# Layer 1's dilated 3x3 convolution by row differences: four products per two output rows, in groups of six rows

## The chip, the cores and the metric

The kernel runs on one core of a Trainium2 chip. The metric is the device time in microseconds of one execution; a kernel's time is the median of several runs. All data are fp32.

## The reference, cut to what matters

Two layers run one after the other on 32 images of 128 channels and 56 x 56 pixels. Layer 0 is a depthwise 7x7 convolution, a layer norm, and a mixture of 8 experts with two experts per pixel and a limited capacity; its result is the image plus the normalized value plus the experts' output. Layer 1, the only one that the change touches, is:

```python
feat = conv2d(x, conv_w, padding=DIL, dilation=DIL)      # 3x3, dilation 3, 128 -> 64 channels
feat = batchnorm(feat, bn1_g, bn1_b, bn1_m, bn1_v)
feat = jax.nn.gelu(feat, approximate=False)
F2 = jnp.fft.fft2(feat.astype(jnp.float32), axes=(-2, -1))
...
attn = complex_softmax(attn)                             # 8 heads of 8 channels
out_f = jnp.abs(jnp.fft.ifft2(out_f, axes=(-2, -1)))
...
gate = cg * F2
gate = jnp.abs(jnp.fft.ifft2(gate, axes=(-2, -1)))
y = jnp.concatenate([out_f, gate], axis=1)
return y + x
```

Output row h of the convolution needs the input rows h - 3, h and h + 3, and in each of them the columns w - 3, w and w + 3.

## The kernel before, in words

Layer 0 writes three things to DRAM: the normalized rows (xf), the experts' outputs in the order of the experts' slots (yf), and, for each pixel, two slot numbers that stay in SBUF. Layer 1 begins when the last expert is done. It works on 16 pairs of images; image pr and image pr + 16 lie in the two halves of the 128 partitions (2 x 64 output channels).

Four parts run in layer 1, written as Python generators whose `yield w` tells how many columns of PE work have just been issued:

- `release` (L428) issues one gather on GpSimd's queue: for 128 pixels, one of the two expert outputs, by an indirect DMA (L444). A gather waits for the PE instruction that was current 16 gathers earlier (`leash`). `total` (L451) adds, for a block of 8 image rows of both images, the two gathered tiles to the tile `xa` by two VectorE additions (L460), and stores the sum to DRAM. Its loads and stores go over SP's queue. `worked` (L468) counts the columns issued and releases a gather per PACE columns (L1510). `bring` (L476) makes sure that a block of rows is summed, which issues what is missing at once, and loads it back.
- `front` (L1264) is the convolution of one pair. `place` (L1249) transposes a block of the sums on PE and adds it to the padded input tile `xp` of each image (L1260); rows of `xp` are RP = 59 elements apart. `taps` (L1267) then issues, for a group of 8 output rows, 9 taps x 2 images of matmuls (L1271) with 448 columns; the two images go to the two halves of the PSUM tile `pf`, so that they use the two column halves of the array. ScalarE applies batch norm and gelu in one pass (L1279).
- `back` (L1339) is all the rest of one pair: the transforms, the attention and the outputs. `transform` (L1306) takes banks of four 128-column blocks: four PE transposes (L1314), a copy of the bank to `mid` on VectorE (L1301), four products with a constant matrix (L1322), and a copy of the result on ScalarE (L1325). It is used four times per pair (rows forward, columns forward, columns back, rows back). `attended` (L1419) and `absolute` (L1483) add the input to the results (L1427, L1490) and store them.
- The main loop (L1512 to L1538) runs `back` of one pair and feeds it steps of the next pair's `front`, in proportion to the work done; the first sixth of `back` gets none except where `back` asks for some. The framework then orders each engine's instructions by estimated readiness, so neighbours in the code can be some places apart on an engine.

[...] PSUM has five banks shared by transposes, products and attention, two for `pf` and one for the Gram matrix.

Lines that the change and the prediction touch: L436 (buffers of `xa`), L485 (loading `xp`), L1230 (the convolution's weights `cw`), L1249 to L1296, L1306 to L1337, L1427, L1490, L1507 to L1510. L1369 is the square root of the Gram matrix's diagonal: it runs once per pair and serves as a mark in time.

Of the kernel before, what the change touches and what calls it, by code (L numbers as in the profile page):

```python
# [30 lines left out]
F32 = mybir.dt.float32  # L31
# [43 lines left out]
def conv_seq_kernel(ctx: ExitStack, tc: tile.TileContext, t: dict, out: bass.AP, dbg: dict):  # L75
# [352 lines left out]
    def release():  # L428

        n = made_["asked"]  # L430
        if n >= NRB * NG:
            return
        made_["asked"] += 1
        r, k = divmod(n, NG)
        if k == 0:
            xs = d6.tile([128, NB, C], F32, name="xa", tag="xa")  # L436
            nc.sync.dma_start(out=xs, in_=xfv[:, r * NB : (r + 1) * NB, :])
            begun_[r] = xs, []
        if k % NB == 0:
            begun_[r][1].append(d6.tile([128, NB, C], F32, name="y"))  # L440
        m = k % NB
        s = (slot1, slot2)[k // NB]
        marks.append(step["pe"])
        gated(marks[max(0, n - leash["n"])], nc.gpsimd.indirect_dma_start(  # L444
            out=begun_[r][1][-1][:, m, :],
            out_offset=None,
            in_=yf[: 1 + reach(r), :],
            in_offset=bass.IndirectOffsetOnAxis(ap=s[:, r * NB + m : r * NB + m + 1], axis=0),
        ))
# [33 lines left out]
        nc.sync.dma_start(out=xs, in_=xsv[:, r * NB : (r + 1) * NB, :])  # L483

    def inputs(pr):  # L485
        xps = [d4.tile([C, XL], F32, name="xp") for i in range(2)]
        for i in range(2):
            nc.sync.dma_start(out=xps[i], in_=t["xp"][pr + i * HI])
        return xps

    def ahead(i, of):

# [23 lines left out]
    if True:  # L516
# [620 lines left out]
        for e in range(E):  # L1137
            todo = late
            chain["on"] = e >= E - 3
            if e + 1 < E:  # L1140
                todo = todo + [due(1.4, lambda e=e: scale(e + 1))]
            if e in pairs:
                todo = todo + search(*pairs[e])
            if e == E - 1:
                for s in late + [left]:
                    s()
                left = lambda: None
                locate()
                lists_.close()
                rkey.__exit__(None, None, None)  # L1150
                d4 = ctx.enter_context(tc.tile_pool(name="d4", bufs=4))
                d6 = ctx.enter_context(tc.tile_pool(name="d6", bufs=6))
                d3 = ctx.enter_context(tc.tile_pool(name="d3", bufs=3))
                first_inputs = inputs(0)
                todo = []
            if e + 1 < E - 1:
                ids2, gates2 = lists()
                steps, late = listing(e + 1, ids2, gates2)
                todo = todo + steps
            elif e + 1 < E:  # L1160
                (ids2, gates2), late = last, []
            if e == E - 4:
                last = lists()
                steps, done_ = listing(E - 1, *last)
                todo = todo + steps + done_
            slots_ = len(chunks) * 4 - 6
            state = [0, 0, 0.0, 0]
            whole = sum(share.get(f, 0.7) for f in todo)

            def tick():  # L1170
                state[0] += 1
                if e == E - 1:
                    state[2] += 1
                    ahead(i, state[2])
                with tc.issue_after(step["dve"].ins):
                    while state[1] < len(todo) and state[2] * slots_ < state[0] * whole:
                        s = todo[state[1]]
                        if s in apart and state[3] == state[0]:
                            break
                        s()  # L1180
                        state[2] += share.get(s, 0.7)
                        state[1] += 1
                        state[3] = state[0]

            for i, c0 in enumerate(chunks):
                if i + 1 < len(chunks):
                    then = fetch(ids, chunks[i + 1], e == E - 1)
                elif e + 1 < E:
                    then = fetch(ids2, 0, e + 1 == E - 1)
                if e in (E - 3, E - 2):  # L1190
                    for n in range(2):
                        if 2 * (i + (e - E + 3) * len(chunks)) + n < NC:
                            put(0, 2 * (i + (e - E + 3) * len(chunks)) + n)
                state[2] = 0 if e == E - 1 else state[2]
                left = expert(e, c0, gates, *now, tick, left)
                now = then
            assert state[1] == len(todo)
            if e + 1 < E:
                ids, gates = ids2, gates2
# [5 lines left out]

    d1 = ctx.enter_context(tc.tile_pool(name="d1", bufs=1))
    d2 = ctx.enter_context(tc.tile_pool(name="d2", bufs=2))
    ring = ctx.enter_context(tc.tile_pool(name="ring", bufs=6))
    psum = ctx.enter_context(tc.tile_pool(name="psum_d", bufs=5, space=PSUM))
    psumf = ctx.enter_context(tc.tile_pool(name="psum_f", bufs=2, space=PSUM))  # L1210
    psum1 = ctx.enter_context(tc.tile_pool(name="psum_g", bufs=1, space=PSUM))
# [16 lines left out]
        return scale, shift  # L1228

    cw = load(d1, "cw", [C, 9, DD], t["conv_w"])  # L1230
    bsc, bsh = batchnorm("bn1")


# [15 lines left out]
    def place(r, xps):  # L1249
        xs, rb = rows.pop(r), r % NB  # L1250
        for m0 in range(0, NB, 4):
# [3 lines left out]
            for m in range(nm):  # L1255
                nc.tensor.transpose(pv[:, :, m, :], xs[:, m0 + m, :], ident)  # L1256
            for i in range(2):
                px = interior(xps[i], rb * P8, P8)[:, :, m0 * P8 : (m0 + nm) * P8]
                pi = pv[:, i * P8 : (i + 1) * P8].rearrange("p r m s -> p r (m s)")
                step["dve"] = nc.vector.scalar_tensor_tensor(  # L1260
                    out=px, in0=pi, scalar=bC, in1=px, op0=ALU.add, op1=ALU.add
                )

    def front(pr, xps, feat):  # L1264


        def taps(pf, g, k0):  # L1267
            for k in range(k0, k0 + 3):
                o = ((k // 3) * 3 + 8 * g) * RP + (k % 3) * 3
                for i in range(2):  # L1270
                    step["pe"] = nc.tensor.matmul(  # L1271
                        pf[i * DD : (i + 1) * DD, : 8 * W],
                        lhsT=cw[:, k, :],
                        rhs=xps[i][:, o : o + 8 * RP].rearrange("p (h w) -> p h w", w=RP)[:, :, :W],
                        start=(k == 0),
                        stop=(k == 8),
                    )
            if k0 == 6:
                nc.scalar.activation(  # L1279
                    feat[:, 8 * g * W : 8 * (g + 1) * W], pf[:, : 8 * W], AF.Gelu, scale=bsc, bias=bsh  # L1280
                )

        bring(pr * NB)
        bring(pr * NB + 1)
        place(pr * NB, xps)
        bring(pr * NB + 2)
        yield NB * 64
        for g in range(NB):
            if g + 1 < NB:
                place(pr * NB + g + 1, xps)  # L1290
                bring(pr * NB + g + 3)
                yield NB * 64
            pf = psumf.tile([128, 512], F32, name="pf")
            for k0 in (0, 3, 6):
                taps(pf, g, k0)
                yield 3 * 8 * W  # L1296

# [3 lines left out]
    act = nc.scalar.copy  # L1303
    K2 = 2 * KF

    def transform(src, n, m, by, to, copy, more=None):  # L1306

        M = by.shape[1]

        def turn(i0):  # L1310
# [2 lines left out]
            for i in range(ni):  # L1313
                step["pe"] = nc.tensor.transpose(pt[:m, i * 128 : (i + 1) * 128], src(i0 + i), ident)  # L1314
            mid = ring.tile([128, 4, 128], F32, name="mid")
            dve(mid[:m, :ni, :].rearrange("p i c -> p (i c)"), pt[:m, : ni * 128])
            return i0, ni, mid

        def product(i0, ni, mid):
# [19 lines left out]
    def back(pr, xps, feat):  # L1339
# [79 lines left out]
        def attended(g):  # L1419
# [1 line left out]
            root = bank("root")  # L1421
            nc.scalar.activation(root[:, : 8 * W], feat[:, 8 * g * W : 8 * (g + 1) * W], AF.Sqrt)
            for i in range(2):
                oa = ring.tile([128, 8 * W], F32, name="oa", tag="o")
                ov = oa[:DD].rearrange("p (h w) -> p h w", w=W)
                rv = root[i * DD : (i + 1) * DD, : 8 * W].rearrange("p (h w) -> p h w", w=W)
                nc.vector.tensor_tensor(out=ov, in0=rv, in1=interior(xps[i], 8 * g, 8)[:DD], op=ALU.add)  # L1427
                nc.sync.dma_start(out=out[pr + i * HI, :DD, 8 * g : 8 * g + 8, :], in_=ov)


# [39 lines left out]
        for i, w in enumerate(  # L1470
            transform(
                lambda k: Z[:, k, :], KF, 4 * KF, ih,
                lambda k, n: T4[:, 2 * k * H : 2 * (k + n) * H], act,
            )
        ):
            if i % 2 and i // 2 < NB:
# [6 lines left out]
        def absolute(at, pm):  # L1483
            j0, nj = at
            nc.scalar.activation(pm, pm, AF.Abs)
            for i in range(2):
                ob = ring.tile([128, 8 * W], F32, name="ob", tag="o")
                ov = ob[DD:].rearrange("p (b j w) -> p b j w", b=2, w=W)
                px = xps[i][DD:, INT0 : INT0 + H * RP].rearrange("p (b j w) -> p b j w", b=2, w=RP)
                nc.vector.tensor_tensor(  # L1490
                    out=ov,
                    in0=pm[i * DD : (i + 1) * DD].rearrange("p (j b w) -> p b j w", b=2, w=W),
# [5 lines left out]

        yield from transform(
            lambda j: T4[:, bass.DynSlice(j, 4 * KF, step=NT)], NT, 4 * KF, iw,  # L1500
            lambda j, n: (j, n), absolute,
        )

    MAIN = 2 * (NT * (64 + 4 * KF) + KF * (64 + 4 * KF)) + NT * 128 + NB * 16 * W + 2 * -(-KF // 4) * 2 * KF
    FRONT = NB * (NB * 64 + 9 * 8 * W)  # L1507
    LEAD = MAIN // 6
    leash["n"] = 16
    PACE = (MAIN + FRONT) / (2 * NP) * 1.07  # L1510
# [152 lines left out]
```

## Time and profile before

| | us |
|---|---|
| median of 3 runs | 5322.87 (5310.27 to 5332.21) |
| the profiled execution, its own time | 5289.68 |
| its span | 5287.9 |
| PE busy in the span | 4697.6 |
| DVE busy | 2808.8 |
| ACT busy | 2112.7 |
| GpSimd (POOL) busy | 2611.9 |
| first and last convolution matmul of layer 1, start | 2988.5 and 5212.8 |

Engines in a profile are PE (TensorE's matmuls), PEld (its weight loads), DVE (VectorE), ACT (ScalarE), POOL (GpSimd) and SP (the queue that issues DMAs). A line such as `L1271 PE MATMUL pf<-xp,cw 128*64 128x448 f32 x4032 | 916.6, 562 | 8.4` reads: line 1271, engine and operation, output and inputs, shape, count, busy time of the group in us, mean length of one in ns, idle time of the engine just before them in us. An fp32 matmul shows as two instructions. PE's ends are modelled, so who reads a PSUM tile tells more about when it was done. "remote" or "unknown queue" marks a wait whose end the records do not attribute.

The busy tenths in 40 slices (132 us each) show layer 0's convolution in the first five slices, the routing and the experts up to slice 22, and layer 1 from slice 23 on.

### The profile page before, as it was taken

The page shows a single profiled execution, that of the slowest core. Times are in us where ns is not written, and L with a number is a line of the kernel's source. Part 1 is how long each engine was busy: PE and PEld are TensorE (multiplying, and loading weights), DVE is VectorE, ACT ScalarE, POOL GpSimd, SP SyncE. Part 2 cuts the span into 40 slices and gives each one's busy share as a digit, 9 for nine tenths or more (in the row PEclk, how much of TensorE's full clock was granted, in tenths as well). Part 3 has the DMA queues.
Part 4 walks back from the last instruction along what each step waited for, and adds up shares of the span by engine and source line. Part 5 has one row for each costly group of instructions (what it writes and reads, how often), then busy time and mean ns, then how long its engine had stood idle before and what let it go on. Part 6 is the DMA issues. An engine that isn't in the chain of part 4 may idle for free.

```text
span 5287.9 us, 87255 instructions
## 1 busy us (share of the span) xinstructions
PE 4697.6 (89%) x32984; PEld 3233.7 (61%) x32984; DVE 2808.8 (53%) x5777; ACT 2112.7 (40%) x4260; POOL 2611.9 (49%) x2633
## 2 busy tenths in 40 slices
PE   8888835999999999999999899989999888888899
PEld 7677724777777777666666455555555554455556
DVE  4787876667676766341112245545545444444456
ACT  3676751444444444443444233333333222222234
POOL 0000022555554555666636666666666666666660
PEclk9999966999999999999999899999999999999999
DMA  9988940222222222333356545555565555555552
GB/s 261 267 258 252 269 110 25 68 63 65 63 67 63 65 66 64 85 91 88 90 165 159 141 120 158 157 153 160 157 163 158 157 159 152 132 150 153 152 147 60
DMA packets 767256, 705.23 MB, mean 133 GB/s; under 512 B 72752, under 2 KB 679089, under 8 KB 762741
## 3 DMA queue, kind: packets, MB, share of 16 engines
q1 hardware_dynamic: 596580, 487.54, 31.1%
q0 software_dynamic: 81664, 167.15, 14.4%
q10 hardware_dynamic: 88592, 44.96, 3.0%
q8 instruction: 262, 4.29, 0.3%
q14 instruction: 158, 1.29, 0.1%
HBM read 472.99 MB, written 226.39 MB: 132 GB/s over the span
## 4 chain that ended last, share of the span: by engine, by line
PE 72%; DVE 10%; ACT 5%; another core or an unknown queue 4%; issue 4%; DMA 3%; POOL 0%; SPq 0%; ACTq 0%; DVEq 0%; POOLq 0%
PE py L1064 17%; PE pf L1271 15%; PE ph L1049 15%; PE pm L1322 9%; PE pt L1314 4%; PE pg L1346 2%; PE pxt L1031 2%; DVE st L196 2%; ACT y L222 2%; DVE y L231 2%; DMA xf<-y 2%; PE psa L171 2%; ACT hT L1052 2%; PE pre L1411 2%
## 5 line engine op out<-in xcount | busy, mean ns | idle before, releaser
L444 POOL DMA_INDIRECT y<-yf,slot x1568 | 1559.3, 994 | 918.8 <-issue 364.2
L1025 POOL DMA_INDIRECT xg<-xf,ids x861 | 907.2, 1054 | 797.9 <-PE ph L1049 510.6
L1052 ACT ACTIVATE hT<-ph,b1t 128x512 f32<-128x512 f32 (+1 forms) x992 | 658.0, 682 | 1219.4 <-PE ph L1049 1048.2
L1064 PEld LDWEIGHTS py<-W,hT 128*128 128x128 f32 x7872 | 967.5, 196 | 242.9 <-ACT hT L1052 139.0
L1064 PE MATMUL py<-W,hT 128*128 128x128 f32 x7872 | 1039.4, 285 | 63.4 <-ACT hT L1052 49.9
L1271 PE MATMUL pf<-xp,cw 128*64 128x448 f32 x4032 | 916.6, 562 | 8.4 <-issue 5.6
L1049 PE MATMUL ph<-xT,W 128*128 128x512 f32 (+1 forms) x1984 | 896.2, 591 | 4.1 <-issue 3.7
L1080 DVE TENSOR_TENSOR yo<-py,b2t 128x512 f32<-128x512 f32 (+2 forms) x256 | 170.7, 669 | 894.6 <-issue 525.7
L1301 DVE COPY mid<-pt 112x512 f32<-112x512 f32 (+3 forms) x480 | 311.1, 662 | 594.8 <-PE pt L1314 228.7
L1049 PEld LDWEIGHTS ph<-xT,W 128*128 128x128 f32 x1984 | 355.5, 191 | 338.2 <-issue 333.7
L1271 PEld LDWEIGHTS pf<-xp,cw 128*64 128x64 f32 x4032 | 283.4, 138 | 437.7 <-issue 398.9
L217 POOL TENSOR_SCALAR y<-y,sd,nb 128x128 f32<-128x128 f32 x49 | 25.5, 540 | 690.8 <-PE plq L263 689.9
L1325 ACT COPY T<-pm 128x464 f32<-128x464 f32 (+2 forms) x240 | 123.5, 520 | 495.2 <-PE pm L1322 315.5
L1090 ACT ACTIVATE yo<-yo,gates 128x128 f32<-128x128 f32 (+1 forms) x984 | 312.4, 394 | 11.4 <-DVE yo L1080 5.7
L222 ACT ACTIVATE y<-y,nb,sd 128x128 f32<-128x128 f32 x735 | 287.5, 481 | 30.9 <-DVE nb L209 30.9
L171 PE MATMUL psa<-xt,stay 112*64 112x98 f32 (+1 forms) x4608 | 230.9, 260 | 39.4 <-DVE y L179 23.6
L1260 DVE SCALAR_TENSOR_TENSOR xp<-pxs,beta,xp 128x256 f32<-128x256 f32 x448 | 173.4, 445 | 154.7 <-PE pxs L1256 47.6
L1322 PE MATMUL pm<-ih,mid 116*128 116x112 f32 x928 | 152.9, 314 | 109.3 <-DVE mid L1301 56.3
L171 PEld LDWEIGHTS psa<-xt,stay 112*64 112x64 f32 (+1 forms) x4608 | 217.4, 145 | 48.4 <-DVE y L179 25.7
L460 DVE TENSOR_TENSOR xa<-xa,y 128x896 f32<-128x896 f32 x224 | 243.4, 1087 | 3.2 <-DVE mid L1301 0.4
L1322 PEld LDWEIGHTS pm<-ih,mid 116*128 116x128 f32 x928 | 131.4, 218 | 180.4 <-DVE mid L1301 59.7
L1279 ACT ACTIVATE feat<-pf,bn_shift,bn_scale 128x448 f32<-128x448 f32 x112 | 81.1, 724 | 401.8 <-remote 152.2
(409 smaller groups left out, 6180.6 us busy)
## 6 DMA issues: line engine op xcount, KB each, us to landing
xt<-in_x_dram SPq DMA_DIRECT2D x256, 392.0 KB
yf<-yo SPq DMA_DIRECT2D x240, 256.0 KB
xp<-in_xp_dram SPq DMA_DIRECT2D x32, 1832.0 KB
xa<-xf SPq DMA_DIRECT2D x112, 448.0 KB
xsum<-xa SPq DMA_DIRECT2D x112, 448.0 KB
xs<-xsum SPq DMA_DIRECT2D x112, 448.0 KB
xf<-y ACTq DMA_DIRECT2D x42, 1024.0 KB
y<-yf,slot POOLq DMA_INDIRECT x1568
```

The costliest lines, as they stand in the source:

```text
L171: nc.tensor.matmul(ps[h * 64 : (h + 1) * 64, c * TG : (c + 1) * TG], lhsT=wts[b][:, c4 + c, :], rhs=xv[: PKS[b], c, h, :, b * NB : b * NB ...
L222: nc.scalar.activation(yi, yi, AF.Identity, scale=sd[:, i : i + 1], bias=nb[:, i : i + 1])
L444: gated(marks[max(0, n - leash["n"])], nc.gpsimd.indirect_dma_start(out=begun_[r][1][-1][:, m, :], out_offset=None, in_=yf[: 1 + reach(r), :],
L460: nc.vector.tensor_tensor(out=xs, in0=xs, in1=y, op=ALU.add)
L1025: paced(q, nc.gpsimd.indirect_dma_start(out=xg[:n, q, :], out_offset=None, in_=xf, in_offset=bass.IndirectOffsetOnAxis(ap=ids[:n, c0 + q : ...
L1049: step["pe"] = nc.tensor.matmul(ph[:, :ns], lhsT=W1[:, e, f * C : (f + 1) * C], rhs=xT[:, :ns], start=True, stop=True)
L1052: gelu = nc.scalar.activation(hT[:, f, :ns], ph[:, :ns], AF.Gelu, bias=b1t[:, e, f : f + 1])
L1064: step["pe"] = nc.tensor.matmul(py[:n, q * C : (q + 1) * C], lhsT=hT[:, f, q * 128 : q * 128 + n], rhs=W2[:, e, f, :], start=(f == 0), sto ...
L1090: nc.scalar.activation(yo[:n, q], yo[:n, q], AF.Copy, scale=gates[:n, c0 + q : c0 + q + 1])
L1271: step["pe"] = nc.tensor.matmul(pf[i * DD : (i + 1) * DD, : 8 * W], lhsT=cw[:, k, :], rhs=xps[i][:, o : o + 8 * RP].rearrange("p (h w) -> ...
L1301: step["dve"] = nc.vector.tensor_copy(to, of)
L1322: step["pe"] = nc.tensor.matmul(pm[:, i * M : (i + 1) * M], lhsT=mid[:m, i, :], rhs=by, start=True, stop=True)
```

## The change

For outputs y(h) and y(h + 3) the four input rows r0 = x(h - 3), r1 = x(h), r2 = x(h + 3) and r3 = x(h + 6) are needed. With the three kernel rows k0, k1 and k2, four products take the place of six:

- m0 = k0 (r0 - r2), m1 = (k0 + k1 + k2)/2 (r1 + r2), m2 = (k0 - k1 + k2)/2 (r2 - r1), m3 = k2 (r3 - r1)
- y(h) = m0 + m1 + m2 and y(h + 3) = m1 - m2 + m3

Each product still has three column taps and runs over three rows at a time (rows h, h + 1, h + 2), so a group is six output rows. A pair has nine such groups and one of the last two rows. Row sums and differences are made on VectorE for both images at once (`lift`), into five buffers; the two mixed kernel rows are made once. PSUM holds m1 and m2 in one bank and m0 and m3 in another; ScalarE copies the first to `feat`, three VectorE operations combine them (m1 is added to both side products, then m2 is added to one and subtracted from the other), and the gelu runs on `feat` in place. Besides, `xp` becomes one tile for both images; `xa` has four buffers instead of six; the output tiles have five buffers of their own instead of six; in the two inverse transforms every second copy to `mid` goes to ScalarE; and FRONT, from which PACE follows, is reckoned anew.

```diff
@@ release
-            xs = d6.tile([128, NB, C], F32, name="xa", tag="xa")
+            xs = d4.tile([128, NB, C], F32, name="xa", tag="xa")
@@ weights, once
+    mixed = d1.tile([C, 2, 3, DD], F32, name="mixed")
+    cu = [cw[:, 0:3, :], mixed[:, 0], mixed[:, 1], cw[:, 6:9, :]]
+    nc.vector.tensor_tensor(out=cu[2], in0=cu[0], in1=cu[3], op=ALU.add)
+    nc.vector.tensor_tensor(out=cu[1], in0=cu[2], in1=cw[:, 3:6, :], op=ALU.add)
+    nc.vector.tensor_tensor(out=cu[2], in0=cu[2], in1=cw[:, 3:6, :], op=ALU.subtract)
+    nc.vector.tensor_scalar(out=mixed, in0=mixed, scalar1=0.5, scalar2=None, op0=ALU.mult)
@@ front
+    SEED = {0: (0, 6, ALU.subtract), 1: (6, 3, ALU.add), 2: (6, 3, ALU.subtract), 3: (9, 3, ALU.subtract)}
-        def taps(pf, g, k0):
-            for k in range(k0, k0 + 3):
-                o = ((k // 3) * 3 + 8 * g) * RP + (k % 3) * 3
-                for i in range(2):
-                    step["pe"] = nc.tensor.matmul(
-                        pf[i * DD : (i + 1) * DD, : 8 * W],
-                        lhsT=cw[:, k, :],
-                        rhs=xps[i][:, o : o + 8 * RP].rearrange("p (h w) -> p h w", w=RP)[:, :, :W],
...
+        def lift(g):
+            n, ms = lines(g)
+            k = n * RP + 3
+            tt = {}
+            for m in (1, 2, 0, 3)[: len(ms)]:
+                tt[m] = d5.tile([128, 2, SL], F32, name="tt")
+                a, b, op = SEED[m]
+                at = [(GR * g + r) * RP for r in (a, b)]
+                step["dve"] = nc.vector.tensor_tensor(
+                    out=tt[m][:, :, :k], in0=xps[:, :, at[0] : at[0] + k], in1=xps[:, :, at[1] : at[1] + k], op=op
+                )
+            return tt
+        def taps(g, tt):
...
+            for pair_ in ((1, 2), (0, 3)):
+                pf = psumf.tile([128, 512], F32, name="pf")
+                for j, m in enumerate(pair_):
...
+                    for k in range(3):
+                        for i in range(2):
+                            step["pe"] = nc.tensor.matmul(
+                                pf[i * DD : (i + 1) * DD, j * 3 * W : j * 3 * W + nw],
+                                lhsT=cu[m][:, k, :],
+                                rhs=tt[m][:, i, 3 * k : 3 * k + n * RP].rearrange("p (h w) -> p h w", w=RP)[:, :, :W],
+                                start=(k == 0),
+                                stop=(k == 2),
+                            )
...
+                nc.scalar.copy(od, mid_)
+                nc.vector.tensor_tensor(
+                    out=side, in0=side, in1=od[:, 0:1].broadcast_to([128, 2, nw]), op=ALU.add
+                )
+                nc.vector.tensor_tensor(out=od[:, 0], in0=side[:, 0], in1=od[:, 1], op=ALU.add)
+                step["dve"] = nc.vector.tensor_tensor(out=od[:, 1], in0=side[:, 1], in1=od[:, 1], op=ALU.subtract)
+            nc.scalar.activation(od, od, AF.Gelu, scale=bsc, bias=bsh)
...
+            lifted.append((g, lift(g)))
+            if len(lifted) == 2:
+                k = lifted.pop(0)
+                taps(*k)
+                yield load_of(k[0])
@@ transform
-            dve(mid[:m, :ni, :].rearrange("p i c -> p (i c)"), pt[:m, : ni * 128])
+            (act if shared and i0 % 8 else dve)(mid[:m, :ni, :].rearrange("p i c -> p (i c)"), pt[:m, : ni * 128])
@@ outputs
-                oa = ring.tile([128, 8 * W], F32, name="oa", tag="o")
+                oa = outs.tile([128, 8 * W], F32, name="oa", tag="o")
@@ pacing
-    FRONT = NB * (NB * 64 + 9 * 8 * W)
+    FRONT = NB * NB * 64 + sum(load_of(g) for g in range(NGR))
```

## The prediction

> **What bounds the kernel now.** I read the page first (engine shares, slices, chain), then the chain by time from 2850 us on, then cut layer 1 into windows at the square root of the norms (L1369, once per image pair, first at 3080.7 us, last at 5230.7), then one stretch of the timeline.
>
> ```profile
> PE 4697.6 (89%) x32984; PEld 3233.7 (61%) x32984; DVE 2808.8 (53%) x5777; ACT 2112.7 (40%) x4260; POOL 2611.9 (49%) x2633
> ...
> PE   8888835999999999999999899989999888888899
> ...
> DVE  4787876667676766341112245545545444444456
> ...
> PE 72%; DVE 10%; ACT 5%; another core or an unknown queue 4%; issue 4%; DMA 3%; POOL 0%; SPq 0%; ACTq 0%; DVEq 0%; POOLq 0%
> ...
> L1271 PE MATMUL pf<-xp,cw 128*64 128x448 f32 x4032 | 916.6, 562 | 8.4 <-issue 5.6
> ```
>
> The convolution pf is the largest piece of PE in layer 1 (slices 23 to 40), and PE holds 72% of the chain.
>
> ```profile
> 3189.10 6.92 PE pf L1271 x36
> ...
> 3543.39 12.54 another core or an unknown queue
> ...
> 5206.79 6.92 PE pf L1271 x36
> ```
>
> 36 instructions in 6.92 us: 192 ns from one to the next (562 is the length of one; two images run side by side in the two column halves). One pair has 7 x 9 x 2 = 126 matmuls, each two instructions: 252 x 192 = 48.4 us.
>
> ```profile
> 2988.50:3080.70 92.20, 81.88 (x433) 42.93 (x434) 23.77 (x52) 12.69 (x20) 58.73 (x61) 0.92 0.49 117
> 3080.70:3898.10 817.40, 750.77 (x4472) 453.39 (x4471) 418.43 (x717) 261.94 (x439) 517.73 (x517) 0.96 0.59 158
> 3898.10:5105.10 1207.00, 1047.83 (x5963) 631.64 (x5962) 569.06 (x969) 348.77 (x585) 771.72 (x779) 0.94 0.57 152
> 5105.10:5230.70 125.60, 122.83 (x747) 74.16 (x745) 64.84 (x115) 43.56 (x74) 27.99 (x30) 0.99 0.30 75
> 5230.70:5287.90 57.20, 46.06 (x295) 34.41 (x293) 40.90 (x70) 30.67 (x56) 0.00 (x0) 0.94 0.24 57
> ```
>
> Columns: length, then busy time of PE, PEld, DVE, ACT, POOL, then granted clock, DMA share, GB/s. Six pairs take 136.2 us each with 86 gathers each (517 / 6), eight take 150.9 with 97 or 98, and the pair that has few gathers left takes 125.6. So PE sets the pace, and gathers with their company cost 10 to 25 us a pair on top. The later pairs are those where the lead in gathers is used up.
>
> ```profile
> 3539.43 6.99 PE L1271 MATMUL pf<-xp,cw 128*64 128x448 f32 x36
> ...
> 3541.18 2.21 DVE L460 TENSOR_TENSOR xa<-xa,y 128x896 f32<-128x896 f32 x2
> ...
> 3541.51 1.57 POOL L444 DMA_INDIRECT y<-yf,slot  x1 [0.30 <-issue]
> ...
> 3547.14 0.94 POOL L444 DMA_INDIRECT y<-yf,slot  x1 [0.30 <-issue]
> ...
> 3552.41 0.72 ACT L1279 ACTIVATE feat<-pf,bn_shift,bn_scale 128x448 f32<-128x448 f32 x1 [13.12 <-remote]
> 3555.95 2.00 DVE L1301 COPY mid<-pt 116x512 f32<-116x512 f32 x3 [12.56 <-remote]
> ```
>
> Two things to see. The activation can read the last pf only at 3552.41, 6 us after the record says that PE was done: the "unknown queue" of the chain is PE itself, slower than its records after a long dense run, with the granted clock at 0.94 on the mean. And a gather takes POOL 0.94 + 0.30 us, but 1.57 under DVE's addition of two SBUF tiles.
>
> [...] The nearest row here is layer 0's convolution, also two column halves:
>
> ```profile
> 319.10 5.50 PEld L171 LDWEIGHTS psa<-xt,stay 112*64 112x64 f32 x128
> ```
>
> 128 loads, each with a matmul of 98 columns, in 5.50 us: 43 ns apiece. So 64-column weights don't hold a short matmul at 98 columns, still less at 168.
>
> **The change part by part.**
>
> PE. Per group of six rows 4 products x 3 taps x 2 images = 24 matmuls of 168 columns; nine groups, and a last one of 18 with 112. That is 216 x 2 = 432 instructions and 36 shorter. Scaling 192 ns by columns gives 72, scaling psa's 43 gives 74; I take 73, and 49 for the short ones: 31.5 + 1.8 = 33.3 us. PE saves 48.4 - 33.3 = 15.1 us a pair, 242 over 16. Bounds: 72 ns saves 15.5; if each load's 138 ns were serial, PE would lose 13 a pair, which psa excludes.
>
> DVE. Added per pair: [...] 9 side additions of 336 elements in PSUM (L1416 has 618 ns for 448, so 0.50), 4.5; 18 additions of 168 and 2 of 112 at about 0.32, 6.4. Removed: 7 of 30 mid copies, 4.4. DVE overlaps neighbours by some 0.08 us per instruction (59 more per pair, 4.9), so DVE goes from 69.7 (418.43 / 6) to about 69.7 + 31.3 - 4.4 - 4.9 = 92 us a pair, from half of the time to three quarters. It lies beside PE. Not everywhere: in the two inverse transforms DVE already writes 28 outputs of 0.62 us and all mid copies, and a difference in front of a mid copy delays the PE products that wait for it. In the changed instruction order most differences stand in fours before and in attention; in the inverse stages single ones stand between copies. I take 2 us a pair, bounds 0 and 10.
>
> ACT. Nine copies of 336 (L1325 has 546 ns for 464, so 0.44) and one short, 4.2; seven mid copies, 3.7; ten gelus for seven, about 1; table loads go from 7 to 10 per pair in the instruction order, 3 x 1.3 = 3.9. ACT rises from 43.7 (261.94 / 6) to 56 us of 125. Hidden, except that ACT now waits for DVE before a gelu, and behind it are the copies of T and Z that PE waits for. Within the 2 us above.
>
> POOL. The number of gathers is the same. Each costs 1.30 us with its issue (996 ns mean + 0.30): 98 are 127 us. Excess over 0.94 is about 5 us a pair now, under 14 additions (L460) and 4 gatings (L1460, 1.12), 19 us of two-input DVE work; the differences add 20 us of that kind, so another 4 to 5. POOL then needs 132 us in a late pair, 116 in an early one. Against PE's 150.9 - 15.1 = 136 this leaves almost nothing. Behind a late gather stand L460's addition in DVE's order, and behind that the copies. I take 4 us in a late pair, bounds 0 and 13.
>
> Pacing. One gather per amount of work, in the same proportion (PACE scales with FRONT), but the first front is shorter work, so the lead starts some 8 gathers smaller; in the changed order 14 additions per pair begin at the sixth interval instead of the seventh. One pair moves from early to late.
>
> Buffers. xa from 6 to 4: rows are 20 us apart, so a store has landed, nothing. Output tiles have five buffers instead of six: up to 1 us in a pair, in the 2 us above. Weights mixed once: four DVE instructions before the first product, under 2 us, beside transposes. SP's DMAs are as many, in the same turn.
>
> Sum: 92.2 - 5 (DVE is busy in the first front: additions, placing, differences) + 5 x (136.2 - 15.1 + 2 = 123) + 9 x (150.9 - 15.1 + 4 = 140) + (125.6 - 15.1 + 1.5 = 112) + 56 = 2130 us where layer 1 has 2299.4. That is 169 less. The profiled execution took 5289.68 us (span 5287.9), 33 under the median of the runs, 5322.87; against that median I get 5153.
>
> **The rivals.**
>
> (a) PE's saving arrives whole[...]. For: 125.6 us in a pair without many gathers, DVE's idle time. Against: POOL's 132. 242 + some 10: 5070. Chance 0.22.
>
> (b) POOL and DVE become the bound of the late pairs: 147 instead of 140, early 130. For: 127 us of POOL stretched to 150.9 already. 87 + 650 + 1323 + 118 + 57 = 2235, 64 less: 5259. Chance 0.21, of which 0.06 reach no change.
>
> (c) Slower: the ring PE, ACT copy, DVE side addition, ACT gelu in every group. [...] while DVE waits for the side product, the mid copies behind it wait, and PE with them. A group saves PE 1.5 us; from 1.5 us of stall per group the change loses. At 2 us, 0.5 x 160 groups = 80 more: 5403. For: waits of PE for mid copies total 55.5 us before pm alone. Against: a group is used one group later, and five PSUM banks lie between. Chance 0.13.
>
> (d) It doesn't do what it says: short matmuls at 138 ns. 5530; psa speaks against it. Chance 0.02.
>
> **How the numbers follow.** Forecast 0.42, with its own range 5110 to 5200. What a measurement can tell from no change is 0.5%, 27 us. Faster: 0.42 + 0.22 + 0.15 = 0.79; same 0.06 and 0.01 of (c), 0.07; slower 0.14. The range goes from 5050, under (a), to 5320, where 0.17 of (b), (c) and (d) stay out above and 0.03 below.
>
> **What would show it.** 432 pf instructions per pair at 73 ns in runs of 24; DVE at 85 to 95 us a pair; early pairs near 123 and late near 140; gathers longer on the mean than 996 ns; POOL over 90% with its issue in late pairs. Wrong if the differences wait in front of mid copies so that PE's idle time before pm doubles, or if pf spacing is over 100 ns.

## The result, and the profile after

The kernel after takes 5509.22 us (median of 4 runs, 5495.98 to 5516.82), the kernel before 5322.03 (4 runs, 5310.27 to 5332.21): a ratio of 1.035, interval 1.032 to 1.038. The change makes it 3.5% slower, where 3% faster was forecast. The later runs fell on four chips (8, 12, 13 and 15 by their numbers; that of this first comparison isn't known). On three of them the kernel before takes 5284 to 5321 us, on number 12 it took 4836, in one run; each run below is therefore compared with its neighbours on the same chip.

The windows of the kernel after, cut as those of before (first product of layer 1, first square root of the norms, pairs, the pair that has few gathers left, the tail; columns as there):

```profile
3014.30:3098.20 83.90, 65.29 (x643) 58.29 (x644) 46.72 (x107) 16.30 (x29) 50.55 (x46) 0.85 0.45 112
3098.20:3833.00 734.80, 608.34 (x4808) 483.58 (x4806) 456.22 (x899) 277.33 (x482) 447.12 (x435) 0.90 0.55 148
3833.00:5327.10 1494.10, 1140.94 (x8651) 904.00 (x8652) 839.10 (x1643) 504.31 (x865) 910.91 (x881) 0.85 0.53 139
5327.10:5439.70 112.60, 106.43 (x955) 85.99 (x954) 83.81 (x172) 56.02 (x97) 16.77 (x16) 1.00 0.30 72
5439.70:5494.20 54.50, 43.24 (x295) 33.35 (x293) 37.05 (x63) 33.67 (x63) 0.00 (x0) 0.97 0.27 60
```

Five pairs take 147.0 us each, nine take 166.0, and the pair with few gathers takes 112.6. Read the fourth row first: with 16 gathers instead of 98, the new convolution gives 112.6 where the old one, with 30, gave 125.6. There the forecast of 112 is met. In the rows with gathers the same work takes up to 53 us longer, and the granted clock falls to 0.85 (before: 0.94). From the first square root to the last the kernel after needs 2341.5 us and before 2150.0: the first five pairs lose 55, the next nine 149, the last gains 13. Another 17 us were lost ahead of the first square root; that is layer 0, which the change doesn't touch and which took 26 us longer in this execution, less 8 us gained in the lead-in.

The page of the kernel after, engine shares, slices and chain:

```profile
PE 4618.8 (84%) x36440; PEld 3557.0 (65%) x36440; DVE 3160.1 (58%) x6757; ACT 2302.2 (42%) x4625; POOL 2662.8 (48%) x2633
...
PE   8888836999999999999987788887778777777879
...
PEclk9999958999999999999999899988888878888889
...
PE 66%; DVE 11%; issue 7%; ACT 7%; another core or an unknown queue 5%; DMA 3%; POOL 0%; SPq 0%; DVEq 0%; ACTq 0%; POOLq 0%
```

PE's busy time is only 79 us less, for an estimated 242 us of removed products, and from slice 23 on it is no longer full: sevens and eights. No other engine is full either, and "issue" and "unknown queue" (together 8% of the chain before) are 12%: time that ends with nobody's recorded work. One stretch of the timeline shows such a piece:

```profile
5075.23 1.93 PE L1316 MATMUL pf<-tt,mixed 128*64 128x168 f32 x24
...
5080.98 0.94 POOL L444 DMA_INDIRECT y<-yf,slot  x1 [0.30 <-issue]
5082.23 0.95 POOL L444 DMA_INDIRECT y<-yf,slot  x1 [0.30 <-issue]
5083.48 0.96 POOL L444 DMA_INDIRECT y<-yf,slot  x1 [0.30 <-issue]
5084.75 0.94 POOL L444 DMA_INDIRECT y<-yf,slot  x1 [0.30 <-issue]
5085.80 0.44 ACT L1332 COPY feat<-pf 128x336 f32<-128x336 f32 x1 [12.72 <-remote]
5086.00 0.94 POOL L444 DMA_INDIRECT y<-yf,slot  x1 [0.31 <-issue]
...
5086.29 1.10 PE L1316 MATMUL pf<-tt,cw 128*64 128x168 f32 x5 [9.13 <-issue]
```

By the records the 24 products of m1 and m2 are done at 5077.16. ACT, whose next instruction is the copy of them, starts it 8.6 us later; PE does nothing for 9.13 us; and all that while POOL issues one gather after the other, 0.30 us apart. That is the pattern that the experiments are about. I call it a late hand-over. Where hand-overs are counted below, the lateness of one is the start of the ACT or DVE instruction that first reads a PSUM bank, less the recorded end of the products in it or of the reader's own last instruction, whichever is later (in layer 1 the banks pf, pt, pm, pre and pim are counted); over 2.5 us it counts as late.

### The profile page after: what moved, and what is told of

Its sections match the earlier page's. It is cut to its first block, busy times and chain, and to the rows that moved or that the text cites. A ratio compares the mean times of both kernels' runs of the same rounds, so it can differ in the third digit from the quotient of the medians.

```text
span 5494.2 us, 95680 instructions
## 1 busy us (share of the span) xinstructions
PE 4618.8 (84%) x36440; PEld 3557.0 (65%) x36440; DVE 3160.1 (58%) x6757; ACT 2302.2 (42%) x4625; POOL 2662.8 (48%) x2633
## 3 DMA queue, kind: packets, MB, share of 16 engines
q0 software_dynamic: 81664, 167.15, 13.7%
## 4 chain that ended last, share of the span: by engine, by line
PE 66%; DVE 11%; issue 7%; ACT 7%; another core or an unknown queue 5%; DMA 3%; POOL 0%; SPq 0%; DVEq 0%; ACTq 0%; POOLq 0%
PE py L1064 16%; PE ph L1049 14%; PE pf L1316 11%; PE pm L1384 8%; PE pt L1376 3%; PE pg L1408 2%; PE pxt L1031 2%; ACT y L222 2%; PE pre L1473 2%; DVE st L196 2%; DVE y L231 2%; PE psa L171 2%; ACT hT L1052 2%; PE pxs L1265 2%
## 5 line engine op out<-in xcount | busy, mean ns | idle before, releaser
L444 POOL DMA_INDIRECT y<-yf,slot x1568 | 1613.0, 1029 | 1061.8 <-issue 363.7
L1316 PE MATMUL pf<-tt,cw 128*64 128x168 f32 (+1 forms) x3648 | 403.2, 341 | 219.6 <-issue 104.6
L1316 PEld LDWEIGHTS pf<-tt,cw 128*64 128x64 f32 x3648 | 300.5, 152 | 288.1 <-issue 154.6
L1316 PE MATMUL pf<-tt,mixed 128*64 128x168 f32 (+1 forms) x3840 | 376.2, 324 | 46.2 <-issue 25.2
L1299 DVE TENSOR_TENSOR tt<-xp 128x360 f32<-128x360 f32 (+1 forms) x624 | 298.9, 518 | 155.8 <-remote 69.3
L1363 DVE COPY mid<-pt 112x512 f32<-112x512 f32 (+2 forms) x368 | 244.9, 668 | 215.3 <-PE pt L1376 83.2
L1316 PEld LDWEIGHTS pf<-tt,mixed 128*64 128x64 f32 x3840 | 278.4, 144 | 138.5 <-issue 87.9
L1332 ACT COPY feat<-pf 128x336 f32<-128x336 f32 x144 | 63.1, 438 | 532.8 <-remote 254.9
```

Source lines behind the costliest of these rows:

```text
L1299: step["dve"] = nc.vector.tensor_tensor(out=tt[m][:, :, :k], in0=xps[:, :, at[0] : at[0] + k], in1=xps[:, :, at[1] : at[1] + k], op=op)
L1316: step["pe"] = nc.tensor.matmul(pf[i * DD : (i + 1) * DD, j * 3 * W : j * 3 * W + nw], lhsT=cu[m][:, k, :], rhs=tt[m][:, i, 3 * k : 3 * k ...
L1363: step["dve"] = nc.vector.tensor_copy(to, of)
```

## The experiments

The theories, by the numbers that the expectations use: (1) the saving is lost only together with the gathers, by the row differences contending with them; (2) the ring PE, ACT copy, DVE addition, gelu stalls; (2') POOL is full, and what waits is waiting for gathers; (3) ACT's copies and table loads (1283 ns each in the traces of before and after) or the fewer buffers cost it; (5) while gathers run, PE's results reach the other engines late, whoever needs the gathers.

**Without gathers, and without either added part.** No gather, zeros in the additions (both kernels):

```diff
-        gated(marks[max(0, n - leash["n"])], nc.gpsimd.indirect_dma_start(
...
+            begun_[r][1].append(made_["zero"])
```

The kernel after without the differences, and, as another run, without the combining operations:

```diff
-                tt[m] = d5.tile([128, 2, SL], F32, name="tt")
...
+                tt[m] = GR * g * RP + SEED[m][0] * RP
...
-                                rhs=tt[m][:, i, 3 * k : 3 * k + n * RP]
+                                rhs=xps[:, i, tt[m] + 3 * k : tt[m] + 3 * k + n * RP]
```

```diff
-                nc.scalar.copy(od, mid_)
-                nc.vector.tensor_tensor(
...
-            nc.scalar.activation(od, od, AF.Gelu, scale=bsc, bias=bsh)
+            nc.scalar.activation(od, mid_[:, :nr], AF.Gelu, scale=bsc, bias=bsh)
```

> Leaves out the gathers of the kernel before: the additions read a tile of zeros instead, everything else stays. Theory 1 (what the change loses is lost only together with the gathers): PE then sets every pair, some 124 us each as in the pair with few gathers, 2990 + 85 + 15 x 123 + 57 = 4980, between 4930 and 5060. Theory 2 (the loss is in the convolution's own ring from PE to ACT to DVE to ACT): the same value; this run is the base for the next one.

> Leaves out the gathers of the kernel after in the same way. Theory 1: the saving of PE arrives: pairs of 108 to 113 us, 4790 in all, at least 150 less than the kernel before without gathers. Theory 2: the ring stalls with or without gathers: pairs of 125 us or more, 4980 or more.

> The kernel after, but the products read the input rows themselves: leaves out the row sums and differences. 20 us of two-input VectorE work a pair are gone, the gathers stay. Theory 1 in the form that the differences contend with the gathers: below 5300, near 5200. Theory 2: the ring stays, so at least 5400. Theory 3 (ACT's copies, table loads, fewer buffers): at least 5400 as well.

> The kernel after, but the gelu reads the bank of m1 and m2 straight from PSUM: leaves out the ACT copy and the VectorE additions that combine the four products. Theory 2 (the ring): below 5300, near 5200. Theory 1 (differences against gathers): 5400 or more, only the 11 us a pair of DVE work from PSUM, which has no second SBUF input, are gone.

Measured, all on the chip where the kernel before takes 4835.68: 4793.49, 4656.14, 4827.41 and 4870.59. Without gathers a good half of the saving arrives: 137 us of the 242, the pairs fall from 121 to 112. (Theory 1 had asked for 150 at least, and 4980 had been expected of the first run, as this chip's time wasn't known.) The other two can't be read without the kernel after beside them, hence the controls:

> The kernel after, unchanged, beside the kernel before, since the kernel before took 4836 us beside the four runs so far and not 5322. Where the kernel before takes about 5320 here, 5500 is expected. Where it takes about 4836: theory 1 (the saving is lost to the gathers on any machine state) expects 4950 to 5010, 3% above; theory 5 (what is lost is late PE work, which the traces at 4836 do not show) expects 4870 to 4890, since the runs without the differences and without the combining additions took 4827 and 4871 and each leaves something out; a saving that arrives would be 4650 to 4700.

> The kernel before, unchanged, for its trace on the same chip as the run beside it. At about 4836 in all: pairs of 121 to 128 us, no granted half clock inside the dense stages, and the activation that reads pf starts where the record of the last pf ends. At about 5320: as in the trace of before that is known.

5476.58 (5466.91 to 5499.91) against 5283.79 (5268.53 to 5302.67), ratio 1.037, interval 1.032 to 1.041; the kernel before with its trace 5272.86. The slow-down is there on a second chip, and with it the late hand-overs. Then the three cut kernels again, beside the kernel after:

> The kernel after without its gathers (the additions read zeros), once more, to stand beside the kernel after of the same call. If the kernel before takes about 5290 beside it: theory 1 (everything that the change loses is lost only while gathers run) expects 4660, as where the kernel before took 4836, since no PE work is then recorded late; a slower chip as such would give 5000 or more.

> The kernel after without the row sums and differences. Where the kernel before takes 4836, POOL ran its gathers back to back all through layer 1 and 4827 came out; the same is expected there. Where the kernel before takes 5290: if the differences beside the gathers are what is lost (theory 1), 5250 or less; if the loss is that each hand-over from PE to ACT and DVE comes late while gathers run (theory 5), 5350 to 5450.

> The kernel after without the ACT copy and the VectorE additions that combine the products: two fewer hand-overs per group. Where the kernel before takes 4836: 4870 again. Where it takes 5290: theory 5 (late hand-overs) 5300 or less, nearer to it than the run without the differences; theory 1, 5400 or more.

> The kernel after, unchanged, with its trace, as the base of the three runs before. Where the kernel before takes 5290: 5480. Where it takes 4836: POOL as the bound (98 gathers of 1.33 us are 130 us a pair) gives 2915 + 15 x 129 + 57 = 4900, about 1% slower than before; PE's saving arriving would give 4700.

Measured, beside 5295.95 for the kernel before: 4732.54, 5372.35, 5385.33 and 5449.76. The gathers cost the kernel after 717 us. Each added part gives back only 1.2 to 1.4% of the kernel's time, where the loss is 2.9% beside it: neither the differences (theory 1 as I first had it, which wanted 5250) nor the ring (theory 2) carries the loss alone. Theory 5 had 5300 or less for the run without the ring, and missed that too. The late pairs without gathers, before on the 4836 chip and after on a 5290 chip:

```profile
3642.90:4614.40 971.50, 971.49 (x5963) 587.00 (x5962) 568.09 (x970) 353.07 (x585) 0.00 (x0) 1.00 0.46 136
```

```profile
3556.20:4568.20 1012.00, 950.28 (x8651) 792.08 (x8650) 826.32 (x1639) 501.26 (x865) 0.00 (x0) 0.99 0.51 149
```

Eight pairs of 121.4 us, all of it PE; nine of 112.4 us, of which PE works 105.6. The pairs without gathers are as long on one chip as on the other (after: 110.7 to 114.9 there, 110.8 to 115.4 here, the last pair aside), so in layer 1 the chips differ only while gathers run.

**Who waits for the gathers, and how long they run on.** A constant in place of the gathered tile in the additions of the kernel after; the leash at 4, and in the same way at 64:

```diff
-                nc.vector.tensor_tensor(out=xs, in0=xs, in1=y, op=ALU.add)
+                nc.vector.tensor_tensor(out=xs, in0=xs, in1=ident[:, None, :].broadcast_to([128, NB, C]), op=ALU.add)
```

```diff
-    leash["n"] = 16
+    leash["n"] = 4
```

> The kernel after with all its gathers, but nobody waits for what they bring: the additions L460 read a constant tile in place of y. If the loss is waiting for gathers (POOL as the bound, theory 2'), it is gone: 4730 to 4780, as without gathers, whichever chip. If gathers that merely run hold up the hand-overs between PE, ACT and DVE (theory 5), 5300 or more where the kernel before takes 5290, and 4730 to 4780 only where it takes 4836.

> The kernel after with the leash at 4 in place of 16: a gather waits for the PE instruction that was current 4 gathers earlier, so POOL runs fewer gathers in one go. Where the kernel before takes 5290: theory 5 (PE's completions stay unseen while a train of gathers runs) expects shorter holds and 5250 or less; theory 2' (POOL's own time is the bound, so any wait of POOL costs) expects 5550 or more. Where the kernel before takes 4836: 4890 or more by both.

> The kernel before with the leash at 4. Where the kernel before takes 5290: theory 5 expects 5150 or less; theory 2' 5330 or more.

> The kernel after with the leash at 64: POOL hardly ever waits for PE. Where the kernel before takes 5290: theory 5 expects longer trains and longer holds, 5500 or more; theory 2' expects 5350 or less, since POOL's waits for PE (218 us in the trace) go.

Measured, beside 5320.8 for the kernel before: 5516.1, 5507.79, 5301.49 and 6052.46. With nobody reading what the gathers bring, the kernel is as slow as ever: on these chips the loss isn't waiting for data (2' falls). A leash of 4 changed nothing, against theory 5, which had wanted 5250 and 5150 or less; but it is no test of short trains, since it made none. A train is a row of gathers with less than 0.45 us between two: counted in the traces, 478 of 1388 gathers of layer 1 stood in trains of 11 or more (leash 16: 553 of 1376, in the control). A leash of 64 is a test of long ones: 1370 of 1372 stood in such trains, and ten late pairs took 200 us each, at a clock of 0.77:

```profile
3878.00:5878.10 2000.10, 1296.82 (x9608) 1009.27 (x9607) 930.59 (x1816) 556.67 (x960) 1009.44 (x971) 0.77 0.43 115
```

POOL's busy time per pair is what it was, 101 us. POOL had more pauses than before, not fewer: 70 us between its trains in a pair of 200, where the control of the kernel after has 38 in 166. What grew is the length of a train, 19 gathers on the mean in place of 6. Letting POOL run so far ahead cost 10% over the kernel after.

**Half the gathers, and the bare products.** Every second call of `release` gathers nothing, and the one gathered tile is added twice; and the kernel after with both cuts from above at once.

```diff
+        m = k // 2
+        s = slot1
         marks.append(step["pe"])
+        if k % 2:
+            return
```

> The kernel after with every second gather left out (only the first expert's output of each pixel is gathered, and added twice), the rest spread as before over the work. Where the kernel before takes 5290: if what costs is that POOL has no pauses (98 gathers of 1.24 us are 122 us of a pair that should take 112), the cost nearly goes: 4750 to 4850, and it is then at least 2.5% faster than the kernel before with half its gathers. If each gather costs the same whatever the pace (700 us for 1394), 5080 to 5110, and no faster than the other.

> The kernel before with every second gather left out in the same way. Where the kernel before takes 5290: no pauses as the cause expects 4900 to 4960 (pairs of 121 to 124 us); a fixed cost per gather expects 5070 to 5090.

> The kernel after without the differences and without the combining additions: all gathers, and of the change only the cheaper products on PE, the mid copies on ACT and the buffers. Where the kernel before takes 5290: if the hand-overs that the change adds carry the loss, the two parts add up (78 and 64 below the kernel after, and more) and PE's saving shows at last: 5200 or less. If a full POOL sets the pace whatever PE saves, the parts don't add up: 5300 to 5370.

Measured, beside 5307.05 for the kernel before: 4827.33, 4883.44 and 5404.23. The late pairs of the first and the second:

```profile
3577.20:4661.60 1084.40, 979.97 (x8653) 815.71 (x8651) 827.76 (x1640) 500.91 (x866) 494.92 (x441) 0.97 0.58 166
```

```profile
3731.40:4703.00 971.60, 971.58 (x5962) 587.04 (x5961) 568.73 (x969) 353.09 (x585) 379.98 (x390) 1.00 0.57 163
```

For the kernel before, 49 gathers a pair are free: 121.5 us, PE full, just as with none. With 98 the pair takes 149.5. For the kernel after 49 cost 8 us and 98 cost 54. So it isn't so much per gather, as the other view had it (5080): it is gathers in long trains. Of the first kernel's 667 gathers in layer 1 from 3000 us on, 539 stand in trains of up to five, and of the second's 664 all do. The expected distance between the two, 2.5%, was 1.1% (one run each). How the hand-over looks with pauses, in the second:

```profile
4367.94 2.48 PE L1274 MATMUL pf<-xp,cw 128*64 128x448 f32 x12
...
4368.28 0.94 POOL L447 DMA_INDIRECT y<-yf,slot  x1 [1.66 <-PE pim L1415]
...
4370.46 0.72 ACT L1282 ACTIVATE feat<-pf,bn_shift,bn_scale 128x448 f32<-128x448 f32 x1 [1.83 <-PE pf L1274]
4370.70 0.94 POOL L447 DMA_INDIRECT y<-yf,slot  x1 [1.48 <-PE pf L1274]
```

The gelu starts 0.04 us after the recorded end of pf. All 112 gelus of that run start within 0.1 us of it.

The controls show where in a train the lateness lies. In that of the kernel before, of the hand-overs whose products ended outside trains 1 of 282 was late, during the first two gathers of a train 9 of 377, later in a train 106 of 637; in that of the kernel after, 0 of 335, 8 of 471 and 116 of 680. A high rate of data isn't what sets it off: the late pairs with full gathers on these chips moved 115 to 153 GB/s, those with half of them, which have few late hand-overs or none, 166 and 163. Whether it is POOL's issuing or the gathers' transfers, no run separates.

The third run was to show whether the added hand-overs carry the loss, and it shows that they don't carry all of it: without any of the added DVE and ACT work of the convolution, and with PE's saving kept, the kernel is still 1.8% slower than before (5200 or less had been one view, 5300 to 5370 the other; it is above both). The two parts don't add up: 1.2 and 1.4% singly; together 1 to 2%, by whether the loss of the kernel after is taken as 2.9% (its one run on this chip) or 3.5 to 3.7% (the two full comparisons). So half of the loss or more is in what is left: fewer and shorter products in 20 PSUM banks a pair instead of 7, but also the copies to mid on ACT, the smaller buffers and the pacing. No run took these apart, so theory 3 is open in this part.

```profile
3794.60:5238.90 1444.30, 1100.32 (x8645) 885.39 (x8644) 606.90 (x1028) 468.81 (x775) 890.57 (x881) 0.87 0.53 144
```

**PE's work put back.** A fourth product for every three taps:

```diff
-                    for k in range(3):
+                    for k, kt in enumerate((0, 1, 2, 2)):
```

> The kernel after with a fourth product per group of three taps: the last column tap is issued and added once more, so PE has 33.3 x 4/3 = 44.4 us of convolution a pair, 11 us more (178 in all), and everything else stays, the pacing of the gathers too. Where the kernel before takes 5290: if the saved PE work had been the cover behind which late hand-overs were hidden, the work put back costs next to nothing: 1.025 to 1.045 of the kernel before, as the kernel after (1.037). If PE's work adds to the path (stalls are the same whatever PE has to do), 1.06 to 1.075. Without gathers it would cost nearly all of the 178.

Measured: 5535.42 (5529.51 to 5554.12) against 5318.12, ratio 1.040, interval 1.035 to 1.046. That is 0.3% over the kernel after (1.037), some 19 us for an estimated 178 us of added PE work; by the two intervals it could be nothing or some 55 us. Its nine late pairs, and its last:

```profile
3859.30:5373.10 1513.80, 1222.87 (x10050) 979.35 (x10049) 847.28 (x1640) 501.57 (x864) 920.61 (x881) 0.89 0.51 138
5373.10:5497.50 124.40, 117.79 (x1120) 99.20 (x1118) 86.33 (x174) 55.44 (x97) 16.24 (x16) 0.99 0.28 68
```

The same 11 us of products cost 8.7 us in the pair with few gathers (124.4 against 115.7 in the control) and 2.1 us in a late pair (168.2 against 166.1). In a late pair PE's idle time shrank by 8.6 us instead. Where gathers ran in long trains, PE's work was nearly free, and so a saving of PE work was worth nearly nothing. The run says one thing more: with 44.4 of the old 48.4 us of products back in each pair, the kernel is still 4.0% slower than before. So the missing PE work isn't what makes the kernel after slower. The slowing comes with the rest of the change.

The late pairs side by side (chips: 12 for before without gathers, 15 for the controls and leash 64, 13 for the work put back, 8 for the others). Idle is length less PE's busy time; late is the time in which at least one hand-over was late, and the next column is PE's idle time within that:

| kernel (us per late pair) | length | PE busy | PE idle | late | idle in it | clock |
|---|---|---|---|---|---|---|
| before, no gathers | 121.4 | 121.4 | 0 | 0 | 0 | 1.00 |
| before, half | 121.5 | 121.4 | 0 | 0 | 0 | 1.00 |
| before (control) | 149.5 | 130.6 | 18.9 | 31.2 | 12.5 | 0.94 |
| after, no gathers | 112.4 | 105.6 | 6.9 | 0 | 0 | 0.99 |
| after, half | 120.5 | 108.9 | 11.6 | 4.0 | 0.9 | 0.97 |
| after (control) | 166.1 | 125.3 | 40.9 | 41.7 | 28.0 | 0.85 |
| after, bare products | 160.5 | 122.3 | 38.2 | 50.8 | 28.4 | 0.87 |
| after, PE work put back | 168.2 | 135.9 | 32.3 | 39.4 | 19.5 | 0.89 |
| after, leash 64 | 200.0 | 129.7 | 70.3 | 68.8 | 47.9 | 0.77 |

Two rows come from these lines of the controls:

```profile
3890.70:5086.60 1195.90, 1044.42 (x5964) 625.91 (x5963) 568.86 (x970) 349.28 (x585) 768.96 (x779) 0.94 0.57 153
```

```profile
3819.30:5314.20 1494.90, 1127.25 (x8652) 879.66 (x8650) 838.60 (x1640) 504.09 (x865) 921.09 (x882) 0.85 0.52 139
```

The full gathers cost before 28 us a pair and after 54. From control to control a late pair changes by 121.4 - 105.6 = 15.8 us less work on PE, 22.0 more idle PE, and 10.5 more for the same work at a slower clock ((125.3 - 105.6) - (130.6 - 121.4)): 16.7 longer together. Of the 22.0, 15.5 lie within late hand-overs, and 6.5 outside, about what the kernel after has without gathers (6.9). In the traces of the first comparison the granted clock stands at half for 14 to 24 us per late pair before and for 41 to 58 after, in stretches of 3.4 us and multiples of it, the longest 13.7 and 23.9 us. With their late pairs divided into stretches of 3.41 us, 118 stretches of the two traces have PE busy for less than half of the time, and the next one stood at half clock after 115 of them; after those with PE busy for 80% or more it did after 19 of 533. So a late hand-over that leaves PE mostly idle costs a second time: PE was busy at half clock for 14.3 us of a late pair before and 35.2 after, and half of that, an estimate of what the slower clock takes, grows by 10.5 here too.

## Why the prediction was wrong

*Right, by its own numbers.* PE's saving (112.6 us in the pair with few gathers, 112 forecast; 71 ns from one product to the next, the median of 106 unbroken runs of 24, for 73), DVE at 92 us a pair (839.1 / 9 = 93.2; the row differences are 20.2 of it, 36 of 360 elements at 527 ns and 3 of 242 at 409, where an estimate on a straight line through 1087 ns for 896 elements, L460, and 618 for 448, L1416, in the trace of before gives 526 and 402), ACT at 56 (504.3 / 9), the tail (54.5 for 56), the lead-in (83.9 for 87). Rival (d) is gone with that. Without gathers the change leaves PE 6.9 us of idle time a pair, for which 2 had been taken within bounds of 0 and 10: that term was too small by 5 us, some 80 in all. Two readings were off without harm: the 192 ns for one old product count the last one's full length, from start to start it is 184, so by this measure the saving is nearer to 14 than to 15.1 us a pair; and DVE gets 61 instructions more per pair, not 59.

*The step that failed* is the term for the gathers, "9 x (150.9 - 15.1 + 4 = 140)" and "5 x (136.2 - 15.1 + 2 = 123)". It took what gathers and their company cost before as a constant that stays when PE has less to do, with 4 us more for POOL, bounds 0 and 13. It isn't a constant. Measured against the pairs without gathers, it went from 28 to 54 us in a late pair, so that late pairs took 166 us instead of 140, and the early ones came to 147 instead of 123.

*Behind it stood a misread line.* The prediction saw the gelu start 6 us after the last pf, with 12.54 us of "unknown queue" in the chain, and put it down to "PE itself, slower than its records after a long dense run". The same dense runs are read within 0.1 us of their end when the gathers have pauses, and no hand-over is late by more than 2.5 us when there are none. So what was late was a hand-over under a train of gathers, and PE's long run alone was not its cause. Before and after have about as many late hand-overs (controls, in layer 1: 116 of 1296 with 516 us together, and 124 of 1488 with 572). But they lie over each other less: they cover 387 us before and 522 after. And after has less work to lay over them: PE is idle for 153 of the 387 us, and for 319 of the 522. That PE's work only fills such time is shown by the work put back (246 of 548). Why the kernel after is then slower than before, and not just as slow, is shown in part: the added DVE and ACT work is 1 to 2% of the kernel's time; a slower clock, 10.5 us a late pair, follows the idle time; what of the rest stretches the lateness is open. Late pairs have 49% of their gathers in trains of 11 or more after and 27% before, which fits, but no run shows which of the two comes first.

*The rivals.* (c) had the sign (5403, 80 us for 187), but its mechanism is a part at most: without the ring the kernel is 1.7% slower than before, and with it 2.9%. (b), POOL as the bound, is not it on the chips of the result, since gathers that nobody waits for cost the same. On the 4836 chip it is what one sees, in the kernel after without differences. Its waits, and its late pairs:

```profile
POOL y L444 <- issue: 276.6, 907, 0.6
DVE xa L460 <- DMA y<-yf,slot: 224.5, 49, 9.1
```

```profile
3374.10:4664.90 1290.80, 1111.46 (x9612) 928.96 (x9611) 761.62 (x1431) 555.40 (x960) 990.27 (x983) 0.92 0.66 179
```

There POOL pauses for 2 us in all ten pairs, its gathers form four trains, no hand-over is late by 2.5 us, and DVE waits for the gathers' data. Ten pairs of 129.1 us with 98 gathers: 1.31 us a gather, which is its 1.007 us and 0.30 of issue. (a), the saving whole, was seen nowhere: without gathers a pair gains 9.0 us of the 15.1.

*Open.* What makes hand-overs late while gathers run on three chips and not on the fourth, and whether that belongs to the chip or to the time of the runs, no run tells. Nor does one tell whether PE then stands still or only its signals are late: the records show both its reader and PE itself waiting, and in the stretch shown PE's signal is recorded 0.02 us before the reader starts, so the reader isn't the slow one. The kernel after as it is was not run on the 4836 chip; by its parts (4827 and 4871 with one part left out) it would be about as fast there as before or a little slower. Spreading all gathers evenly over layer 1, or doing with fewer POOL instructions, was not tried. No kernel of the study that computes everything was faster than the kernel before by more than 0.4% (leash 4 in the kernel before, one run).

## What to carry to other kernels

Before pricing less work on the engine that is the bound, ask what its work was hiding, and look for a stage that has the company and one that hasn't: here one pair with 16 gathers said 112 and the others said 166. When the bound engine gets faster, everything that must keep up with it has less room: 98 gathers of 1.24 us (0.94 and 0.30) are 122 us, which fit with pauses into a pair of 150 us and not into one of 112. A line such as "unknown queue" at the end of a dense run is a wait without an owner, and has to be explained by a run before a forecast is built on it.

## What the runs showed of the hardware that was not expected

- While GpSimd issued gathers in long trains, results of PE reached ACT and DVE late, up to 23 us after PE's recorded work (control of the kernel after, at 3896 us; in the traces of the first comparison 29 of ACT's 112 first readings of pf were late before, by up to 10.3 us, and 52 of 160 after, by up to 13.1). This was so on three chips with the kernel after, on one of them (number 15) with the kernel before, and in layer 0's experts too (20 of 992 hand-overs in the trace of before). It was not seen once over 2.5 us on a fourth, in two cut kernels whose gathers had still fewer pauses. The kernel before is 9 to 10% slower on those chips (5284 to 5321 against 4836).
- With half the gathers, spread out, POOL's company cost the kernel before nothing at all: 121.5 us a pair, as with none.
- An estimated 178 us of additional PE work cost some 19 us.
